# Scan rows behind the routing, first blocks' rows in the sorted rows' places, a last store on GpSimd, attention's additions later and in halves

## The chip, the cores and the metric

The kernel runs on one core of one Trainium2 chip. The metric is the time of one execution on the device in microseconds (us), the median of several runs. One core has a matrix engine (TensorE, PE in the profile, with its weight loads as PEld), a vector engine (VectorE, DVE), an engine for activation functions (ScalarE, ACT), a general engine (GpSimd, POOL) and one that issues transfers (SyncE, SP). Each works through its own list of instructions in order, and they meet through semaphores.

## The reference

The input x has 8 batches of 512 tokens with 256 numbers each, all float32. Four parts follow one another, each added to what went in:

```python
x = x + scan(layernorm(x))        # silu(x Win + b), a state that decays by 0.9, times Wout
x = x + ffn(layernorm(x))         # mixture of experts
x = x + attention(layernorm(x))   # causal, 16 heads of 16
x = x + ffn(layernorm(x))         # the same mixture of experts, same weights
```

```python
def ffn(x):
    topk_idx, tw = _route(x, router_w, bias)            # 4 of 16 experts for each token
    combine = (one_hot(topk_idx, E) * tw[..., None]).sum(1)
    h = einsum('td,edf->etf', x, gate_w)
    u = einsum('td,edf->etf', x, up_w)
    y = einsum('etf,efd->etd', silu(h) * u, down_w)
    routed = einsum('etd,te->td', y, combine)
    sh = silu(x @ sh_gate_w) * (x @ sh_up_w) @ sh_down_w    # shared experts, all tokens
    return routed + sh
```

The routing takes sigmoid scores, keeps the two best of four groups of experts, the four best experts in them, and scales the four scores to a sum of 2.5.

## The kernel before

Tokens lie on the 128 partitions, so a batch is a tile of 128 x 4 x 256. There are four long stages. The first (0 to 368 us) runs over the 8 batches with the scan (class Scan, L436), the routing of the batch before and the shared experts of the batch before that. The second (368 to 769) runs the routed experts in blocks of 128 sorted rows (routed, L765; 136 blocks). The third (769 to 1350) is the attention (class Attention, L965) with routing and shared experts of the second mixture in the same manner, the fourth (1350 to 1749) its blocks. Then the last sums go out, to 1776.

**Order inside a batch.** stretch (L1192) sets the order by hand. Each piece of work is a generator; beside takes a step from the piece that is least far, and timed gives a piece's steps the share of the batch at which each falls due. So a batch's instructions are one list, merged from the main product (pz, state, y, py in the scan), the normalizations, the routing (scores, choices), the sends of the rows and the shared experts. Tiles come from pools with a number of places per tag; an instruction that needs a place waits until the tile that had it before has been read.

**The routing's rows.** normed (L376) takes the mean and the variance of a batch on VectorE (L382, L383), raises the variance to the power -0.5 on GpSimd (L402), or on VectorE where by_vector is set, calls place for the tile, and writes four normalized row tiles on VectorE (L405). For the routing, place (L524) takes a tile of tag rows (two places; 4 x 272 numbers for a partition) and writes the token's number into its last columns with an iota on GpSimd (L526). So the iota waits until the transfers that read the tile's last holder have landed. These transfers are the sends (L665): 16 indirect transfers for each batch, issued by GpSimd, that put the rows where their experts' blocks begin to be read (xg). They follow the gain (L651), which VectorE writes into the same tile after the scores' product pr.

**The scan's chain.** For each of four columns of a batch PE makes pz, ScalarE its sigmoid, VectorE the product xi (L476), the running state (L478) and, after ScalarE's multiplication of xi, the output y (L482). The output product py (L421) needs the four y. All these stand on VectorE in one list with the rows of L405.

**The boundary.** The last shared sum of a stage is copied by ScalarE (L947) and stored by SP (L948). Then each engine loads a count (L889) and branches (L892): more blocks than 136 run only where they are needed. In this data they are not, and the untaken side adds to the semaphores what the taken side would have added, on SP and on GpSimd too. Then run (L869) loads the rows of the first two blocks (load, L792; SP's transfer at L796), and PE turns them (L811). The rows' tiles are in tag kb4 (nine places), which the shared experts, the transposes and many more share.

**The attention's inputs.** After the first mixture, x of a batch is the sum of two parts: the residual with every other block's sums, and the shared experts' with those of the rest. load_sum (L140) issues both loads on SP and one addition of 128 x 1024 on VectorE (L145). In a batch of the stretch it is called after the pieces of the routing are made and before beside merges them, so the addition stands at the head of the batch's list. The attention runs two batches ahead: when it starts, batches 0 and 1 lie ready (prepared, L1132), made beside the blocks, and batch 2 is loaded in its first batch. Its main product begins with pq, whose copies with a parity mask stand on VectorE (L1002).

Of the kernel before, what the change touches and what calls it, by code (L numbers as in the profile page):

```python
# [10 lines left out]
FP = mybir.dt.float32  # L11
AF = mybir.ActivationFunctionType
ALU = mybir.AluOpType
AX = mybir.AxisListType

P = 128
B, T, D = 8, 512, 256
# [57 lines left out]
def tile_hybrid_block(  # L75
# [64 lines left out]
    def load_sum(i: int, b: int, more, queue=nc.sync):  # L140

        x_sb = xpool.tile([P, NT, D], FP, tag="x", name=f"x{i}_{b}")
        queue.dma_start(out=x_sb, in_=rows_of(parts[i][0], b))
        queue.dma_start(out=more, in_=rows_of(parts[i][1], b))
        nc.vector.tensor_add(x_sb, x_sb, more)  # L145
        x_tiles[b] = x_sb


# [226 lines left out]

    def normed(b: int, tag: str, place, by_vector: bool = False):  # L376

# [26 lines left out]
        for t in range(NT):  # L404
            nc.vector.tensor_scalar(  # L405
                xn[:, t, :], x_sb[:, t, :], mv[:, t, 0:1], rstd[:, t : t + 1], ALU.subtract, ALU.mult
            )
            yield
# [24 lines left out]
    class Scan:  # L433
# [3 lines left out]

        norms, scores, choose = (0.08, 0.2, 0.32, 0.4), (0.48, 0.52, 0.61, 0.66), (0.71, 0.97)

        def load(self, b: int):  # L440
# [70 lines left out]

    counts = [region, region]
    upto = {}

    class Route:
# [8 lines left out]
        def place(self):  # L524
            rows = work.tile([P, NT, ROW], FP, tag="rows", name=f"sorted_{self.tag}")
            nc.gpsimd.iota(  # L526
                rows[:, :, D + 2 * TK :].bitcast(I32), [[P, NT], [0, 8]], base=self.b * T, channel_multiplier=1
            )
            self.held["rows"] = rows
            return rows[:, :, 0:D]  # L530

        def norm(self, by_vector: bool = False):
            return normed(self.b, self.tag, self.place, by_vector)

# [26 lines left out]
    def choices(i: int, b: int, tag: str, held, paced: bool):  # L561
# [81 lines left out]
        if not paced:  # L643
# [6 lines left out]
        nc.vector.reciprocal(den, den)  # L650
        nc.vector.scalar_tensor_tensor(  # L651
            rows[:, :, D : D + TK], gain, ROUTE_SCALE, den.unsqueeze(2).to_broadcast([P, NT, TK]), ALU.mult, ALU.mult
# [112 lines left out]
    def routed(i: int, table, beside):  # L765
# [3 lines left out]
        PE, SP = mybir.EngineType.PE, mybir.EngineType.SP  # L769
        held = {}  # L770

# [20 lines left out]
        def load(n: int):  # L792
            if n not in held:
                values(n)
            rows = work.tile([P, 4 * D], FP, tag="kb4", name=f"rows_{i}_{n}", bufs=KB)
            nc.sync.dma_start(out=rows[:, 0:ROW], in_=xg[i][bass.ds(held[n][1], BLK), :])  # L796
            held[n].append(rows)
# [70 lines left out]

        def run(first: int, last: int):  # L869
            load(first)  # L870
            load(first + 1)
            fetch(first)
            turn(first)
            for n in range(first, last + 2):
                if n + 2 < last:
                    load(n + 2)
                if n + 1 < last:
                    fetch(n + 1)
                if n < last:
                    up(n)  # L880
                if n + 1 < last:
                    turn(n + 1)
                if n - 2 >= first:
                    down(n - 2)
                    for work_beside in beside.get(n - 1, ()):
                        work_beside()
# [9 lines left out]
    def shared_experts(i: int, b: int, xnT_of, tanh: bool):  # L896
# [3 lines left out]
        def steps():  # L900
# [32 lines left out]
            for half in range(2):  # L933
# [13 lines left out]
                nc.scalar.copy(y_sb[:, 2 * half : 2 * half + 2, :], py)  # L947
            nc.sync.dma_start(out=rows_of(parts[i][1], b), in_=y_sb)  # L948

# [14 lines left out]
    class Attention:  # L964
        mixture, ahead, copies = 1, 2, by_both  # L965
        early = 2
        norms, scores, choose = (0.0, 0.12, 0.2, 0.28), (0.42, 0.46, 0.55, 0.6), (0.66, 0.95)

        def end(self):
# [3 lines left out]
        def load(self, b: int):  # L973
            load_sum(0, b, kb4(f"more0_{b}"))

# [156 lines left out]
    def prepared(b: int):  # L1132
# [17 lines left out]
        def begin():  # L1150
            x_sb = xpool.tile([P, NT, D], FP, tag="x", name=f"x0_{b}")
            more = free_home("v", f"more_{b}")
            for j, dst in ((1, more), (0, x_sb)):
                nc.gpsimd.dma_start(out=dst, in_=rows_of(parts[0][j], b))
            held.update(x=x_sb, more=more)

        def add():
            for t in range(0, NT, 2):
                rows = held["x"][:, t : t + 2, :]
                tc.keep_in_program_order(nc.vector.tensor_add(rows, rows, held["more"][:, t : t + 2, :]))  # L1160
            x_tiles[b] = held["x"]
            steps.append(normed(b, f"l1_{b}", place, by_vector=True))
# [29 lines left out]
    def stretch(layer):  # L1192
# [41 lines left out]
        for b in range(B):  # L1234
# [16 lines left out]
            if b > 0:  # L1251
                r = start_route(b - 1)
                if last:
                    pieces.append(timed(r.norm(), *spread(0.0, 0.12, NT), *spread(0.2, 0.28, NT)))
                else:
                    first, then, rows, full = layer.norms
                    pieces.append(timed(r.norm(), *spread(first, then, NT), *spread(rows, full, NT)))
# [12 lines left out]
            if nxt < B:  # L1270
                layer.load(nxt)
                pieces += [
                    timed(norm(nxt), *spread(0.32, 0.44, NT), *spread(0.56, 0.64, NT)),
                    timed(turn(nxt), 0.75, 0.79),
                ]
# [167 lines left out]
```

## Time and profile before

| what | us |
|---|---|
| median of 3 runs (1785.84 to 1786.67) | 1786.35 |
| the profiled execution | 1778.1 |
| its span | 1776.4 |
| PE busy in 0 to 50 | 28.50 |
| PE busy in 50 to 265 | 206.49 of 215 |
| PE busy in 265 to 300 | 26.33 of 35 |
| PE busy in 300 to 368 | 65.79 of 68 |
| PE busy in 368 to 375 | 0.88 of 7 |
| PE busy in 375 to 769 | 393.48 of 394 |
| PE busy in 780 to 790 | 1.39 of 10 |
| PE busy in 800 to 1349 | 538.81 of 549 |
| PE busy in 1349 to 1356 | 0.78 of 7 |
| PE busy in 1356 to 1749 | 391.91 of 393 |
| PE busy in 1749 to 1776.4 | 0.80 of 27.4 |

The page shows one profiled execution; the span is from its first to its last instruction. A group's row names line, engine, operation, what it writes and reads, and in brackets how long the engine idled before it and what ended that wait. A row of waits has the waiting engine and line, the one it waited for, total us, times and the longest. A row of windows has, after the window and its length, the busy time of PE, PEld, DVE, ACT and POOL with the instructions in brackets, then the granted clock of PE as a share of full speed, the share of the transfer engines and GB/s. A row of the timeline has the start and the duration in us.

### The profile page before, as it was taken

The page shows a single profiled execution, that of the slowest core. Times are in us where ns is not written, and L with a number is a line of the kernel's source. Part 1 is how long each engine was busy: PE and PEld are TensorE (multiplying, and loading weights), DVE is VectorE, ACT ScalarE, POOL GpSimd, SP SyncE. Part 2 cuts the span into 40 slices and gives each one's busy share as a digit, 9 for nine tenths or more (in the row PEclk, how much of TensorE's full clock was granted, in tenths as well). Part 3 has the DMA queues.
Part 4 walks back from the last instruction along what each step waited for, and adds up shares of the span by engine and source line. Part 5 has one row for each costly group of instructions (what it writes and reads, how often), then busy time and mean ns, then how long its engine had stood idle before and what let it go on. Part 6 is the DMA issues. An engine that isn't in the chain of part 4 may idle for free. (4 is left out here: it accounts for less than half of the span.)

```text
span 1776.4 us, 32812 instructions
## 1 busy us (share of the span) xinstructions
PE 1674.7 (94%) x10640; PEld 1253.8 (71%) x10640; DVE 1090.5 (61%) x3399; ACT 805.7 (45%) x1740; POOL 772.2 (43%) x675
## 2 busy tenths in 40 slices
PE   5999998989999999979999999999998999999994
PEld 3566664579999999954445455455466999999993
DVE  5977767435555655545776675766753665555552
ACT  2322222135555555535654554544523555555552
POOL 4255554625555655530021422312452555555663
PEclk9999998999999999989999999999999999999997
DMA  5443322535555655530012112112443555566766
GB/s 168 161 152 128 131 91 91 184 76 96 95 98 108 103 98 94 98 83 13 25 50 73 63 61 73 52 58 78 145 177 79 94 98 94 103 134 128 129 123 178
DMA packets 149998, 181.37 MB, mean 102 GB/s; under 512 B 16096, under 2 KB 136960, under 8 KB 149824
## 3 DMA queue, kind: packets, MB, share of 16 engines
q0 software_dynamic: 54432, 81.53, 24.1%
q1 hardware_dynamic: 93600, 93.50, 17.3%
q10 hardware_dynamic: 1792, 4.19, 0.6%
q8 instruction: 89, 1.46, 0.3%
q14 instruction: 85, 0.70, 0.1%
HBM read 81.62 MB, written 97.53 MB: 101 GB/s over the span
## 5 line engine op out<-in xcount | busy, mean ns | idle before, releaser
L859 POOL DMA_INDIRECT part<-rows x272 | 428.3, 1575 | 363.6 <-ACT rows L858 287.4
L665 POOL DMA_INDIRECT xg<-sorted_m,slots_m x256 | 256.5, 1002 | 279.4 <-ACT slots_m L662 115.5
L822 PEld LDWEIGHTS ph<-rows,gate 128*128 128x128 f32 x2176 | 285.9, 192 | 15.8 <-ACT rows L812 1.1
L822 PE MATMUL ph<-rows,gate 128*128 128x128 f32 x2176 | 289.3, 276 | 0.6 <-ACT rows L812 0.6
L822 PE MATMUL ph<-rows,up 128*128 128x128 f32 x2176 | 288.5, 276 | 0.0
L850 PE MATMUL pyr<-w_all,rows 128*128 x1088 | 280.4, 380 | 0.0
L822 PEld LDWEIGHTS ph<-rows,up 128*128 128x128 f32 x2176 | 266.0, 193 | 0.0
L830 ACT ACTIVATE rows<-ph 128x256 f32<-128x256 f32 x272 | 104.5, 384 | 328.7 <-PE ph L822 328.7
L831 DVE TENSOR_TENSOR rows<-ph,rows 128x256 f32<-128x256 f32 x272 | 115.3, 424 | 194.1 <-ACT rows L830 193.8
L850 PEld LDWEIGHTS pyr<-w_all,rows 128*128 128x128 f32 x1088 | 185.2, 191 | 14.2 <-ACT rows L858 0.4
L804 ACT COPY gate<-w_all 128x512 f32 x272 | 170.1, 627 | 14.7 <-SPq L892 2.5
L1057 ACT ACTIVATE w_all<-ps_a 128x1024 f32<-128x1024 f32 x128 | 124.4, 1021 | 80.2 <-PE ps_a L1046 74.1
L804 DVE COPY up<-w_all 128x512 f32 x272 | 119.5, 440 | 33.3 <-PE ph L822 18.1
L858 ACT ACTIVATE rows<-pyr,gain 128x256 f32<-128x256 f32 x272 | 128.6, 473 | 14.4 <-PE pyr L850 12.2
L1046 PE MATMUL ps_a<-w_all 32*128 32x512 f32 (+3 forms) x1024 | 122.1, 472 | 7.1 <-ACT w_all L1057 5.7
L911 PE MATMUL pg_m<-xT_m,su_sb 128*128 128x512 f32 x256 | 126.6, 617 | 0.8 <-DVE sig_m L929 0.8
L835 DVE SCALAR_TENSOR_TENSOR gain<-rows,expert_b 128x4 f32<-128x4 f32 x272 | 61.2, 225 | 103.8 <-ACT rows L858 84.2
L911 PE MATMUL pg_m<-xT_m,sg_sb 128*128 128x512 f32 x256 | 123.0, 603 | 0.0
L939 PE MATMUL pd_m<-sd_sb,act_m 128*128 128x256 f32 x512 | 120.5, 384 | 0.0
L832 DVE TENSOR_TENSOR rows<-ph,rows 128x256 f32<-128x256 f32 x272 | 115.1, 423 | 8.3
L811 PE MATMUL pt<-ident,rows 128*128 128x128 f32 x544 | 105.0, 275 | 13.4 <-DMA rows<-xg 13.1
L939 PEld LDWEIGHTS pd_m<-sd_sb,act_m 128*128 128x128 f32 x512 | 96.1, 191 | 21.1 <-issue 4.7
(219 smaller groups left out, 2203.0 us busy)
## 6 DMA issues: line engine op xcount, KB each, us to landing
rows<-xg SPq DMA_DIRECT2D x272, 136.0 KB, 2.6
part<-x SPq DMA_DIRECT2D x16, 512.0 KB, 3.0
part<-ys_m SPq DMA_DIRECT2D x16, 512.0 KB, 3.0
w_all<-in_L_ffn_gate_w_dram SPq DMA_DIRECT2D x24, 256.0 KB, 5.4
w_all<-in_L_ffn_up_w_dram SPq DMA_DIRECT2D x24, 256.0 KB, 4.8
w_all<-in_L_ffn_down_w_dram SPq DMA_DIRECT2D x24, 256.0 KB, 5.6
sum<-part POOLq DMA_DIRECT2D x10, 512.0 KB, 3.9
xg<-zeros SPq DMA_DIRECT2D x34, 136.0 KB, 2.3
```

Of the source, the lines that this page charges most:

```text
L665: nc.gpsimd.indirect_dma_start(out=xg[i], out_offset=bass.IndirectOffsetOnAxis(ap=slots[:, at : at + 1], axis=0), in_=rows[:, t, :], in_of ...
L804: copy(here, w_all[:, bass.ds(held[n][0] + half * KD * F, KD * F)])
L822: nc.tensor.matmul(ph[:, s, f * P : (f + 1) * P], lhsT=both[s][:, k * F + f * P : k * F + (f + 1) * P], rhs=rows[:, ROW + k * P : ROW + (k ...
L831: nc.vector.tensor_mul(act, ph[:, 0, :], act)
L832: nc.vector.tensor_mul(act, ph[:, 1, :], act)
L850: nc.tensor.matmul(py, lhsT=act[:, f * P : (f + 1) * P], rhs=w_all[:, bass.ds(w + 2 * KD * F + f * D, D)], start=(f == 0), stop=(f == KF - 1),
L858: nc.scalar.mul(rows[:, 0:D], py, gain[:, TK : TK + 1])
L859: nc.gpsimd.indirect_dma_start(out=parts[i][n % 2], out_offset=bass.IndirectOffsetOnAxis(ap=rows[:, D + 2 * TK : D + 2 * TK + 1].bitcast(U ...
L911: nc.tensor.matmul(dst, lhsT=w[:, k, f * P : (f + 1) * P], rhs=xnT[:, k, :], start=(k == 0), stop=(k == KD - 1),)
L939: nc.tensor.matmul(py[:, j, :], lhsT=acts[n][:, f, t * P : (t + 1) * P], rhs=shared[n][3][:, f, :], start=(n == 0 and f == 0), stop=(n == ...
L1046: nc.tensor.matmul(ps[j // 2][:, j % 2, col : col + n], lhsT=k_sb[w][r, o, c * P : (c + 1) * P], rhs=q_sb[r, o, c * P : T], start=True, st ...
L1057: nc.scalar.activation(es[two], ps[two][:, :, 0:cols], AF.Exp, scale=ATT_SCALE)
```

## The change

Five edits:

- normed takes a function past. For the routing of the first mixture it gives the instruction that wrote the gain of the batch before (L651, kept in gained), and each of the four rows of L405 is issued after it in the order. For the first batch and for the second mixture there is nothing to stand behind. The iota of place keeps its place in program order, which puts it after the power on GpSimd.
- In the last batch of a stretch the rows fall due at last_rows: 0.26 to 0.33 in the scan; in the attention 0.2 to 0.28, as before.
- The first two blocks of each run take their rows' tiles from tag rows, the sorted rows' places; the others from kb4 as before.
- The shared sum of the last batch is stored by GpSimd, the others' by SP.
- load_sum issues the loads (the shared part first) and returns the addition as two steps of 512 columns; in the attention's stretch these fall due at 0.24 and 0.28 of the batch. prepared uses the same function on GpSimd's queue.

The diff, without the import of nullcontext:

```diff
@@ -140,10 +140,18 @@
     def load_sum(i: int, b: int, more, queue=nc.sync):
 
         x_sb = xpool.tile([P, NT, D], FP, tag="x", name=f"x{i}_{b}")
+        queue.dma_start(out=more, in_=rows_of(parts[i][1], b))
         queue.dma_start(out=x_sb, in_=rows_of(parts[i][0], b))
-        queue.dma_start(out=more, in_=rows_of(parts[i][1], b))
-        nc.vector.tensor_add(x_sb, x_sb, more)
         x_tiles[b] = x_sb
+
+        def added():
+
+            for t in range(0, NT, 2):
+                rows = x_sb[:, t : t + 2, :]
+                tc.keep_in_program_order(nc.vector.tensor_add(rows, rows, more[:, t : t + 2, :]))
+                yield
+
+        return added()
 
 
     load_x(0)
@@ -373,7 +381,7 @@
     by_both = (nc.scalar.copy, nc.vector.tensor_copy)
     by_scalar = (nc.scalar.copy, nc.scalar.copy)
 
-    def normed(b: int, tag: str, place, by_vector: bool = False):
+    def normed(b: int, tag: str, place, by_vector: bool = False, past=lambda: None):
 
         x_sb = x_tiles[b]
         stats = small.tile([P, NT, 6], FP, tag="stats", name=f"stats_{tag}")
@@ -402,9 +410,10 @@
             nc.gpsimd.tensor_tensor(rstd, rstd, neg_half, ALU.pow)
         xn = place()
         for t in range(NT):
-            nc.vector.tensor_scalar(
-                xn[:, t, :], x_sb[:, t, :], mv[:, t, 0:1], rstd[:, t : t + 1], ALU.subtract, ALU.mult
-            )
+            with tc.issue_after(past().ins) if past() is not None else nullcontext():
+                nc.vector.tensor_scalar(
+                    xn[:, t, :], x_sb[:, t, :], mv[:, t, 0:1], rstd[:, t : t + 1], ALU.subtract, ALU.mult
+                )
             yield
 
     def kb4(name: str):
@@ -436,6 +445,7 @@
 
 
         norms, scores, choose = (0.08, 0.2, 0.32, 0.4), (0.48, 0.52, 0.61, 0.66), (0.71, 0.97)
+        last_rows = (0.26, 0.33)
 
         def load(self, b: int):
             if b + 1 < B and b > 0:
@@ -510,6 +520,7 @@
         return sel
 
     counts = [region, region]
+    gained = {}
     upto = {}
 
     class Route:
@@ -523,14 +534,19 @@
 
         def place(self):
             rows = work.tile([P, NT, ROW], FP, tag="rows", name=f"sorted_{self.tag}")
-            nc.gpsimd.iota(
-                rows[:, :, D + 2 * TK :].bitcast(I32), [[P, NT], [0, 8]], base=self.b * T, channel_multiplier=1
+            tc.keep_in_program_order(
+                nc.gpsimd.iota(
+                    rows[:, :, D + 2 * TK :].bitcast(I32), [[P, NT], [0, 8]], base=self.b * T, channel_multiplier=1
+                )
             )
             self.held["rows"] = rows
             return rows[:, :, 0:D]
 
         def norm(self, by_vector: bool = False):
-            return normed(self.b, self.tag, self.place, by_vector)
+
+
+            past = (lambda: gained.get(self.b - 1)) if self.i == 0 else lambda: None
+            return normed(self.b, self.tag, self.place, by_vector, past=past)
 
         def scores(self):
             yield from turned(
@@ -648,7 +664,7 @@
         nc.vector.tensor_reduce(den, gain, AX.X, ALU.add)
         nc.vector.tensor_scalar(den, den, 1e-20, None, ALU.add)
         nc.vector.reciprocal(den, den)
-        nc.vector.scalar_tensor_tensor(
+        gained[b] = nc.vector.scalar_tensor_tensor(
             rows[:, :, D : D + TK], gain, ROUTE_SCALE, den.unsqueeze(2).to_broadcast([P, NT, TK]), ALU.mult, ALU.mult
         )
 
@@ -767,7 +783,7 @@
         weight_at, row_at, expert, many, _ = table
         ACT, DVE = mybir.EngineType.Activation, mybir.EngineType.DVE
         PE, SP = mybir.EngineType.PE, mybir.EngineType.SP
-        held = {}
+        held, first_of = {}, [0]
 
         def values(n: int):
 
@@ -792,7 +808,12 @@
         def load(n: int):
             if n not in held:
                 values(n)
-            rows = work.tile([P, 4 * D], FP, tag="kb4", name=f"rows_{i}_{n}", bufs=KB)
+            if n - first_of[0] < 2:
+
+                rows = work.tile([P, NT, ROW], FP, tag="rows", name=f"rows_{i}_{n}")
+                rows = rows.rearrange("p t c -> p (t c)")[:, 0 : 4 * D]
+            else:
+                rows = work.tile([P, 4 * D], FP, tag="kb4", name=f"rows_{i}_{n}", bufs=KB)
             nc.sync.dma_start(out=rows[:, 0:ROW], in_=xg[i][bass.ds(held[n][1], BLK), :])
             held[n].append(rows)
 
@@ -867,6 +888,7 @@
             )
 
         def run(first: int, last: int):
+            first_of[0] = first
             load(first)
             load(first + 1)
             fetch(first)
@@ -945,7 +967,8 @@
                             )
                     yield NSH * KF * D
                 nc.scalar.copy(y_sb[:, 2 * half : 2 * half + 2, :], py)
-            nc.sync.dma_start(out=rows_of(parts[i][1], b), in_=y_sb)
+
+            (nc.gpsimd if b == B - 1 else nc.sync).dma_start(out=rows_of(parts[i][1], b), in_=y_sb)
 
         return Piece(NSH * KF * (2 * KD * T + NT * D), steps())
 
@@ -965,13 +988,14 @@
         mixture, ahead, copies = 1, 2, by_both
         early = 2
         norms, scores, choose = (0.0, 0.12, 0.2, 0.28), (0.42, 0.46, 0.55, 0.6), (0.66, 0.95)
+        last_rows = (0.2, 0.28)
 
         def end(self):
             for e in range(first_expert, E):
                 load_expert(e)
 
         def load(self, b: int):
-            load_sum(0, b, kb4(f"more0_{b}"))
+            return load_sum(0, b, kb4(f"more0_{b}"))
 
         def project(self, b: int, xnT):
             tag = f"a{b}"
@@ -1148,17 +1172,11 @@
 
 
         def begin():
-            x_sb = xpool.tile([P, NT, D], FP, tag="x", name=f"x0_{b}")
-            more = free_home("v", f"more_{b}")
-            for j, dst in ((1, more), (0, x_sb)):
-                nc.gpsimd.dma_start(out=dst, in_=rows_of(parts[0][j], b))
-            held.update(x=x_sb, more=more)
+            held["added"] = load_sum(0, b, free_home("v", f"more_{b}"), nc.gpsimd)
 
         def add():
-            for t in range(0, NT, 2):
-                rows = held["x"][:, t : t + 2, :]
-                tc.keep_in_program_order(nc.vector.tensor_add(rows, rows, held["more"][:, t : t + 2, :]))
-            x_tiles[b] = held["x"]
+            for _ in held["added"]:
+                pass
             steps.append(normed(b, f"l1_{b}", place, by_vector=True))
 
         def step(many: int):
@@ -1251,7 +1269,7 @@
             if b > 0:
                 r = start_route(b - 1)
                 if last:
-                    pieces.append(timed(r.norm(), *spread(0.0, 0.12, NT), *spread(0.2, 0.28, NT)))
+                    pieces.append(timed(r.norm(), *spread(0.0, 0.12, NT), *spread(*layer.last_rows, NT)))
                 else:
                     first, then, rows, full = layer.norms
                     pieces.append(timed(r.norm(), *spread(first, then, NT), *spread(rows, full, NT)))
@@ -1268,7 +1286,9 @@
                         timed(some(r.rest, PICKS), *spread(*layer.choose, PICKS)),
                     ]
             if nxt < B:
-                layer.load(nxt)
+                added = layer.load(nxt)
+                if added is not None:
+                    pieces.append(timed(added, 0.24, 0.28))
                 pieces += [
                     timed(norm(nxt), *spread(0.32, 0.44, NT), *spread(0.56, 0.64, NT)),
                     timed(turn(nxt), 0.75, 0.79),
```

## The prediction

> **What bounds the kernel now.** I read the page's first two parts, then TensorE's waits, then the windows of the stages, then each stall in order of time.
>
> ```profile
> span 1776.4 us, 32812 instructions
> PE 1674.7 (94%) x10640; PEld 1253.8 (71%) x10640; DVE 1090.5 (61%) x3399; ACT 805.7 (45%) x1740; POOL 772.2 (43%) x675
> ```
>
> TensorE is busy for 1674.7 of 1776.4 us. No edit touches a matmul, so what can be won is its 101.7 us of idle time, and the slow clock after an idle stretch. The waits of PE say who ends that time (total, times, longest):
>
> ```profile
> PE pt_l L368 <- DVE xn L405: 16.0, 4, 15.0
> PE pt L811 <- DMA rows<-xg: 13.1, 4, 6.2
> PE py_s L421 <- DVE y_s L482: 9.2, 6, 2.0
> PE pl_m L549 <- ACT xT_m L370: 9.2, 2, 7.5
> PE pt_l L368 <- DVE w_all L1002: 8.6, 1, 8.6
> ...
> PE pt_m L368 <- DVE sorted_m L405: 3.9, 2, 2.1
> ```
>
> The first row is nearly all the kernel's start (15.0), untouched. The others are the change's targets: two boundaries into the experts' blocks (13.1), the scan's output product (9.2), the last scan iteration (7.5 of 9.2), the first attention batch (8.6). The page's chain of waits starts at 1353 us, so it says nothing of the first three stages. In the windows the columns that matter are PE busy and PEclk, the granted clock:
>
> ```profile
> 265.00:300.00 35.00, 26.33 (x80) 15.20 (x79) 21.72 (x67) 9.41 (x23) 15.47 (x16) 0.80 0.23 86
> ...
> 780.00:790.00 10.00, 1.39 (x9) 1.01 (x12) 3.28 (x9) 0.61 (x2) 0.00 (x0) 0.63 0.53 164
> 790.00:800.00 10.00, 8.57 (x42) 2.68 (x40) 5.43 (x15) 6.56 (x8) 2.20 (x3) 0.86 0.00 1
> ```
>
> The two places of low clock are those after the two longest stalls. Two timelines of VectorE show the head of each queue:
>
> ```profile
> 191.03 1.38 DVE L405 TENSOR_SCALAR sorted_m<-x,mv_m,rstd_m 128x256 f32<-128x256 f32 x4 [7.18 <-POOL rstd_m L402]
> ...
> 786.72 1.23 DVE L145 TENSOR_TENSOR x<-x,more 128x1024 f32<-128x1024 f32 x1 [12.48 <-DMA more<-part]
> 787.87 0.75 DVE L1002 TENSOR_SCALAR w_all<-pq_a,parity 128x512 f32<-128x512 f32 x1
> ```
>
> In both, ready work stands behind an instruction that waits.
>
> **What the Trainium skill says.** "Advanced Engine Details and Errata", Sequencer and Instruction Queues: an engine's instructions go into one queue and there wait for their semaphores; the trace agrees (12.48 us of wait, L1002 behind it). "TensorE: Matmul & The Clock Gate", What's actually happening: the array falls to half clock after an idle window of about 3.4 us and needs a busy one to recover; the trace agrees in kind (8.61 us idle, then 0.63 and 0.86). "DMA: Bandwidth & Descriptors", Issuing engines are not separate DMA queues: issuing from another engine saves only the issue time on the sequencer; here 0.38 us on SP, 0.83 us on GpSimd for the same 512 KB (L1154). The price of the halved addition: "VectorE: DVE Perf Modes", the TRN2 errata, gives (N+151)/0.96 ns for a float32 tensor_tensor, so 1.22 us at 1024 and 0.69 at 512; the trace has 1.23, and 0.68 at 512 (L930).
>
> **Part 1, attention's additions.** Before, load_sum puts the 1024-wide addition of x0_2 at the point where its loads are issued. Those follow the last scatter-adds of the experts, so VectorE stands from 774.2 to 786.72. Behind it is L1002 (0.75 us), and PE, having reached its transposes at 780.05, waits for it until 788.67: 8.61 us. After, the additions are a piece due at 0.24 to 0.28 of the batch. In the order after, L1002 comes directly after the L1002 ahead of it, at 774.2, and the first half of x0_2's addition stands behind the L1002 that ran at about 806, so at about 798 once the stall is gone. The data lands at 786.7, 11 us before: no wait. Cost: six additions become twelve, 6 x (2 x 0.68 - 1.23) = 0.8 us of an engine that is 61% busy, hidden beside PE. The clock: 10 us at 0.86 is up to 1.4 us; I take 0.5, as ScalarE holds PE there too (6.56 us busy). Later batches: VectorE's other waits for x<-part (15.8 us in 5) go, but PE idles there 0.1 to 0.5 us each: 0 to 2 us, taken as 0. Part 1: -9 (bounds -7.5, -12).
>
> **Part 2, scan rows behind the routing.** Before, in an iteration (the one from 183.4, period 40.72 us), VectorE has the variance at 183.85 and waits 7.18 us: GpSimd is sending the rows of an earlier batch to 188.10, its iota (L526) waits for these to land until 189.81, then comes the power to 190.99. All of the scan's work is queued behind the four rows. After, the rows follow the gain of the batch before (L651), one at each step, and the iota comes after the power and after the first sends. I stepped the new VectorE order through the measured durations, with PE where it was:
>
> - Without rows ahead, the first xi starts at 186.03, not 192.33. The routing's sums then wait for PE's pr (190.83) and ScalarE (191.14), so 0.8 us of the 6.3 are lost; the gain ends at 198.87 instead of 204.4, 5.5 us earlier.
> - Then xi_3, row 1 (0.35), state_3 (1.22), rows 2 to 4, to 202.72; y_3 at 202.71 to 203.46, earlier than 208.59.
> - PE wants the rows' transposes at 201.0 to 201.4 and waits some 1.4 us there; its old wait of 1.75 us for y_3 (206.9 to 208.65) is gone. Net -0.35 in the two steady iterations; the fourth gains 1.2 (it had 0.85 and 1.75), the third loses 0.9 (it had 0.55), the second loses 1.5 (it had none). Together -0.5 for five iterations. Each hand-made position is good to about 1 us, so -4 to +5; I take 0.
>
> Last iteration: VectorE waits 7.25 us for the rows' rstd at 272.44, its first xi is at 273.74; PE stands from 278.94 to 286.45 (7.51 us, pl_m for ScalarE's xT_m copies, which stand in ScalarE's queue behind products of the scan). After, VectorE runs 6.3 us earlier; rows end at about 282.7, PE transposes to 283.2, and xT_m, now behind xi_3's product, comes at 284.5: PE starts pl 2.0 us earlier, with its idle time cut in pieces. In that stage 35 us at a clock of 0.80 hold some 4 us of slow matmuls (14 pl in 3.01 us against 1.85 elsewhere); I take 0.5 of it. So -2.5 (bounds 0, -5).
>
> Behind it: sorted_m0_7 waited 3.33 us on VectorE for the last send of m0_5 to land (about 314.2; sends 286.56 to 307.80), PE then 2.06 us (312.8 to 314.9), and a slow clock (8 transposes in 2.21 us against 1.04). These sends hang on the gain and start some 6 us earlier, so land at 308, before rstd at 310.9. -2.06 and 0.5 of clock: -2.5 (bounds 0, -3.5). Part 2: -5 (bounds -9, +5).
>
> **Part 3, the two boundaries.** Before: PE ends at 368.32, ScalarE's copy at 368.95, SP's store to 369.35, SP's TensorLoad L889 at 369.4, branch 369.7, its semaphores to 370.5, L782 some 1.1 us, the first rows' load at 372.07, landed 374.42; PE idle 6.12 us, 6.22 at the second (load 1353.43). After, the store and its wait stand on GpSimd, and SP reaches the load early. But rows_0 and rows_1 now lie in the tag of the sorted rows, which GpSimd's sends read and which the untaken branch's blocks also use: the load waits for GpSimd's semaphore increment at that branch's end, and GpSimd is behind the store. Its chain: copy 368.95, store 0.83, TensorLoad 0.33 to 0.76, branch 0.3, increment 1.0 to 1.6 (the rows of L892): 371.4 to 372.4, around 372.0. That is what SP took. Gain 0 to 0.7 each; I take 0.4. If GpSimd's increment counts at its start the load goes at 370.4: -1.6 each; if GpSimd's branch is slower than SP's, +0.7. Part 3: -1 (bounds -3.5, +1.5). The tail from 1749 on (27.4 us) is untouched.
>
> **Sum.** -9 -5 -1 = -15 on the profiled execution (1778.1 us, 1.7 of it outside the span): 1763. That one is 8.25 us (0.46%) below the median 1786.35; taken off the median, 1771.3, say 1771.5.
>
> **Rivals.**
> - Attention only: the rows' wait on PE takes back what the scan gains, GpSimd's increment takes what SP gives up. For: 1.4 us in each iteration stands on a hand-made position. Against: the last iteration's stall hangs on VectorE's 7.25 us. 1786.35 - 9 = 1777.4.
> - More: clock and stalls of 265 to 315 all recovered (-9) and boundaries free of GpSimd (-3 each): -24, 1762.5. For: SP's path holds 3 us after the copy. Against: the chain above.
> - Slower: the rows behind the gain starve PE. Place: PE's transposes at 201 in each iteration. If the gain stays at 204.4, because the routing's sums hang on PE and ScalarE rather than on the rows ahead, the rows end at 208.3 and PE waits 7.3 us instead of 1.75: 5 x 5.5 = 28, plus 2 at the last iteration, less 10: +20, 1806. It decides from 3 us per iteration on (5 x 3 = 15), a gain at 201.9. Against: before, pr and ScalarE are ready at 191, 13 us ahead of the gain.
> - No change: the addition still waits at its new place (a later landing) or L1002 is held by another wait, scan neutral: 1785.
>
> **Chances.** Forecast 0.54 (own range 1767 to 1775.5), attention only 0.24, more 0.11, slower 0.06, no change 0.05. About 0.2% (3.6 us) is what a measurement can tell. Faster 0.89, same 0.05, slower 0.06. The range to hold 8 in 10 covers the forecast, most of attention only and a part of more: 1763 to 1780.
>
> **What would show it.** Right: no VectorE wait over 2 us for x<-part at the start of attention, PE's wait for L1002 gone; sorted_m's wait for rstd_m (39.8 us in 9) nearly gone, pt_m's wait for sorted_m grown from 3.9 to about 8, py_s's for y_s from 9.2 to under 2; pl_m's 7.5 at about 5; the first load still some 3 us after the last copy, with GpSimd's increment just ahead of it. Wrong: pt_m's wait above 20, or the idle time at 780 elsewhere by another name.

## The result, and the profile after

The changed kernel takes 1766.89 us (median of 4 runs, 1764.67 to 1771.96) against 1786.14 for the one before: a ratio of 0.9893 with a 95% interval of 0.9878 to 0.9909, so 19.3 us (16 to 22) less. The forecast was 1771.5, within 1763 to 1780; the narrower range of the outcome that was called the forecast began at 1767, just above what was measured.

The head of the changed kernel's page:

```profile
span 1766.9 us, 32836 instructions
PE 1678.8 (95%) x10640; PEld 1254.8 (71%) x10640; DVE 1094.7 (62%) x3405; ACT 808.3 (46%) x1740; POOL 776.5 (44%) x677
```

Its waits of PE (engine and line that wait, what for, total us, times, longest; the lines of the code have moved by 8 to 24):

```profile
PE pt_l L376 <- DVE xn L414: 17.0, 4, 15.5
PE pt L832 <- DMA rows<-xg: 15.6, 8, 5.8
PE pt_m L376 <- DVE sorted_m L414: 9.8, 8, 3.2
...
PE py_s L430 <- DVE y_s L492: 3.0, 2, 2.0
PE pl_m L565 <- ACT xT_m L378: 2.1, 2, 1.7
```

The 8.6 us for L1002 is gone, pl_m's 9.2 is 2.1, and py_s's 9.2 is 3.0; pt_m's wait for the sorted rows has grown from 3.9 to 9.8. The loads of the rows cost more in all than before, with four more waits, though the longest is shorter: of that below.

The span changed by 9.5 us in these two profiles and the median by 19.3, so the whole must be cut before it is read. Here it is cut at PE's own instructions (the first pz of an iteration, the last pd_m of a stage, the first pt of the blocks, the first pv of an attention batch), in us, with a second profile of the kernel before (before_again, span 1786.6) beside it:

| stretch | before | before_again | after |
|---|---|---|---|
| start to the third iteration | 63.87 | 64.72 | 65.99 |
| third to last iteration | 200.95 | 202.03 | 199.50 |
| last iteration to the stage's end | 103.50 | 102.19 | 96.58 |
| first boundary, PE idle | 6.12 | 6.11 | 5.79 |
| first blocks, to attention's first pv | 401.56 | 402.45 | 401.53 |
| first attention batch | 49.52 | 49.49 | 39.29 |
| six batches | 357.39 | 357.45 | 357.43 |
| last batch to the stage's end | 166.75 | 167.10 | 168.80 |
| second boundary, PE idle | 6.22 | 6.13 | 5.26 |
| second blocks | 393.91 | 398.19 | 399.05 |
| tail | 26.56 | 30.74 | 27.66 |

The five stretches that the change was to act on give 1.45 + 6.92 + 0.33 + 10.23 + 0.96 = 19.9 us (19.5 against before_again). The others give back 10.4 in this pair of profiles and nothing (-0.2) against before_again, so most of the 10.4 differs from run to run. The medians, 19.3 us apart, lie beside the 19.9.

### The profile page after: what moved, and what is told of

Its sections match the earlier page's. It is cut to its first block, busy times and chain, and to the rows that moved or that the text cites. A ratio compares the mean times of both kernels' runs of the same rounds, so it can differ in the third digit from the quotient of the medians.

```text
span 1766.9 us, 32836 instructions
## 1 busy us (share of the span) xinstructions
PE 1678.8 (95%) x10640; PEld 1254.8 (71%) x10640; DVE 1094.7 (62%) x3405; ACT 808.3 (46%) x1740; POOL 776.5 (44%) x677
## 4 chain that ended last, share of the span: by engine, by line
PE 46%; DMA 4%; issue 1%; DVE 1%; ACT 1%; POOL 1%; ACTq 0%; SPq 0%; POOLq 0%; DVEq 0%
PE ph L843 13%; PE pyr L871 6%; PE pg_m L933 5%; PE ps_a L1070 5%; PE po_a L1105 4%; PE pd_m L961 2%; PE pq_a L1015 2%; PE pt L832 2%; PE pv_a L1033 2%; PE py_a L430 2%; DMA part<-rows 1%; DMA xg<-sorted_m,slots_m 1%; PE pl_m L565 1%; PE pto_a L1121 1%; POOL xg L681 1%
```

## The experiments

The runs fall in three groups. Each group ran on one chip, with the kernel before beside it: 1802.87 us in the first, 1784.26 in the second, 1787.15 in the third. Ratios are to that one; they and their intervals stand as on record, and the quotient of the medians can differ from them by 0.002. Only stretches of the same chip are compared, unless it is said otherwise; of the kernel before there is a trace in the second group alone.

**1. The parts, each alone, and the whole again (first group).** In attn_only, the kernel before gets the new load_sum and its timed steps (due at 0.24 and 0.28 of the batch) alone; two lines of the diff:

```diff
-        nc.vector.tensor_add(x_sb, x_sb, more)
+        return added()
```

> Only the attention's additions of the change (later, in halves, the shared part loaded first), all else as before. Theory: the head of VectorE's list is what PE waits for at the start of attention, so the 8.6 us wait for L1002 goes and the clock after it stays up; in the changed kernel's trace the first attention batch was 10.2 us shorter, so 9 to 10.5 us less than before, scan and boundaries unmoved. Rival (the loads are late anyway and the wait returns under another name in that batch): under 4 us less.

Ratio 0.9921 (0.9891 to 0.9951): 14 us less, with an interval of 5 to either side that takes in the 9 to 10.5 expected. The first attention batch takes 39.28 us, as in the changed kernel, where bound_only and scan_only, without this part, take 49.34 and 49.59 on this chip. The rival falls. The later place, the halves and the order of the two loads were not tried apart.

In scan_only, past, the iota's place and last_rows alone:

```diff
+            past = (lambda: gained.get(self.b - 1)) if self.i == 0 else lambda: None
+            return normed(self.b, self.tag, self.place, by_vector, past=past)
```

> Only the scan's part: rows behind the gain, iota in program order, the last batch's rows at 0.26 to 0.33. Theory: VectorE's wait for GpSimd's power was at the head of its list; the last scan iteration and what follows it give nearly all, 6 to 7 us, the iterations before about 0.8 us each where PE had 1.75 and now has 0.84, less about 1 us each where it had none: 6 us less than before in all, with a spread of 2 from the start. Rival (PE waits for the rows instead of y, a zero sum): within 1.5 us of before.

0.9955 (0.9930 to 0.9979): 8 us less (4 to 13), where 6 were expected. Third to last iteration: 199.49, against 204.10 in attn_only and 203.65 in bound_only, so the stretches show 4 to 5 of the 8. But the last iteration to the stage's end took 110.35, and 110.64 and 110.03 without the scan's part. On this chip that stretch is some 7 to 13 us longer than on the others in every kernel, and nothing is won in it, although its long wait falls here too, from 6.75 us to pieces of 3.19, 1.00 and 0.46. The waits behind it are of the same kind with and without the scan's part (pd_m for act_m, pr_m for sel_m); why this chip has them is open.

In bound_only, the first two blocks' tiles and the last store alone:

```diff
-            nc.sync.dma_start(out=rows_of(parts[i][1], b), in_=y_sb)
+            (nc.gpsimd if b == B - 1 else nc.sync).dma_start(out=rows_of(parts[i][1], b), in_=y_sb)
```

> Only the first two blocks' places and the last store on GpSimd. Theory: GpSimd's increment after the untaken branch gates the first load, so PE's idle time at the boundaries falls from 6.12 and 6.22 to about 5.8 and 5.3: 1.3 us less in all. Rival (SP's list was the gate, and is free now): both idle times below 4 us, 5 us less or more.

1.0007 (0.9992 to 1.0022). PE idles 5.70 and 5.16 us: 1.4 less together than in attn_only (6.11 and 6.16), too little for these runs to show. The rival falls: neither idle time is below 4 us, and 5 us would have shown.

> The changed kernel once more, unedited. In its first trace the second experts' stage took 399.0 us against 393.9 before, with four waits of PE for rows<-xg between 1585 and 1628. If that stretch belongs to the change, it is here again and the time is near 1768; if it is chance of the transfers, it is shorter or elsewhere, and the time is near 1764.

0.9905 (0.9875 to 0.9936); on this slower chip the expected 1768 and 1764 can't be told apart by the time. The second blocks took 399.29 us again, and the waits are back. PE's timeline of after_again:

```profile
1605.83 0.41 PE L832 MATMUL pt<-ident,rows 128*128 128x128 f32 x2 [0.35 <-DMA rows<-xg]
1610.08 0.41 PE L832 MATMUL pt<-ident,rows 128*128 128x128 f32 x2 [1.19 <-DMA rows<-xg]
1643.76 0.41 PE L832 MATMUL pt<-ident,rows 128*128 128x128 f32 x2 [1.93 <-DMA rows<-xg]
1647.44 0.41 PE L832 MATMUL pt<-ident,rows 128*128 128x128 f32 x2 [0.62 <-DMA rows<-xg]
```

The stage starts at 1360.46 here and at 1340.18 in the first trace, so these stand 245 to 287 us behind its start, as they do there (1585 to 1627). In iota_only the four are at the same places. The other kernels have waits for rows near these places too, but fewer or shorter ones: one of 0.53 us in the kernel before, one of 1.93 in before_again, two in bound_only, three in scan_only. The four profiles whose iota stands as before (two of the kernel before, attn_only, bound_only) have 393.9 to 398.2 us in this stage (mean 395.7). Four with the iota in program order (the changed kernel twice, scan_only, iota_only) have 396.4 to 399.3 (mean 398.3); six more, which change the boundary further, have 397.7 to 403.3. So perhaps 2.6 us of the gain are given back late in the second blocks. The ranges overlap, and the kernel before in its second profile is within 0.9 us of the changed one, so this is not shown. By what way an iota's place in the attention's list, or in the scan's, could reach a load of rows there was not tried and stays open.

**2. What holds the first load at a boundary (second group).** Before, SP was late, behind its own store and branch:

```profile
368.97 0.38 SPq L948 DMA_DIRECT2D part<-ys_m  x1
372.07 7.17 SPq L796 DMA_DIRECT2D rows<-xg  x9
374.44 0.66 PE L811 MATMUL pt<-ident,rows 128*128 128x128 f32 x2 [6.12 <-DMA rows<-xg]
```

In the changed kernel, the timeline of all engines shows who is late:

```profile
362.11 0.59 ACT L969 COPY ys_m<-pd_m 128x512 f32<-128x512 f32 x1 [1.53 <-PE pd_m L961]
362.99 0.92 POOL L971 DMA_DIRECT2D part<-ys_m  x1 [10.49 <-ACT ys_m L969]
...
365.50 3.73 SPq L817 DMA_DIRECT2D rows<-xg  x5
367.84 0.22 DVE L856 SCALAR_TENSOR_TENSOR gain<-rows,expert_b 128x4 f32<-128x4 f32 x1 [3.70 <-DMA rows<-xg]
367.87 0.66 PE L832 MATMUL pt<-ident,rows 128*128 128x128 f32 x2 [5.79 <-DMA rows<-xg]
```

and the rows of the branch's line (count, shortest, median and longest in ns, first and last start in us) give GpSimd's part of it:

```profile
L914 SPq EVENT_SEMAPHORE  x16: 17/17/17, 343.1 to 1316.8; - x16
...
L914 POOLq INC_SWDGE_SEM  x2: 654/828/1002, 364.3 to 1336.7; - x2
```

SP is through the branch at 343, 19 us before PE ends. GpSimd's increment starts at 364.3 and takes 1.00 us, and SP's load goes at 365.50, 0.2 us behind it. Three edits tell the tie apart. First, the rows in kb4, with the store still on GpSimd:

```diff
-            if n - first_of[0] < 2:
-                rows = work.tile([P, NT, ROW], FP, tag="rows", name=f"rows_{i}_{n}")
-                rows = rows.rearrange("p t c -> p (t c)")[:, 0 : 4 * D]
-            else:
-                rows = work.tile([P, 4 * D], FP, tag="kb4", name=f"rows_{i}_{n}", bufs=KB)
+            rows = work.tile([P, 4 * D], FP, tag="kb4", name=f"rows_{i}_{n}", bufs=KB)
```

> The changed kernel with all blocks' rows in tag kb4 again, the store still on GpSimd. Theory: the place in tag rows is what ties the first load to GpSimd's increment; without it the load waits for nothing of GpSimd, goes when PE ends, and PE's idle time at a boundary falls from 5.8 and 5.3 to some 3 us; but rows_1 gets the place of the last sum, so it waits for that store to land (issue 363.0, some 4.3 us), and gives about 1 us of it back as a second wait. 2 to 5 us less than the changed kernel. Rival (the branch on the other engines is the gate): idle times unchanged, same time.

PE's timeline:

```profile
358.72 2.11 PE L956 MATMUL pd_m<-sd_sb,act_m 128*128 128x256 f32 x9
364.20 0.66 PE L827 MATMUL pt<-ident,rows 128*128 128x128 f32 x2 [3.37 <-DMA rows<-xg]
368.33 0.66 PE L827 MATMUL pt<-ident,rows 128*128 128x128 f32 x2 [3.47 <-DMA rows<-xg]
```

The first wait falls to 3.37 us (2.24 at the second boundary). Without the place in tag rows nothing of GpSimd holds it: the load goes at 360.86, as PE ends, and GpSimd's increment starts only at 363.05. But the second block's rows now have the last sum's place, and wait until its store has landed: 3.47 and 4.39 us more, where about 1 was expected. Ratio 0.9893 (0.9869 to 0.9918), the same as the changed kernel's in the result (it did not run in this group), and not the 2 to 5 us less that were expected. Second, each block where it is free:

```diff
-            if n - first_of[0] < 2:
+            if n - first_of[0] == 1:
```

> The changed kernel with only the second block's rows in tag rows, the first block's in kb4. Theory: the first load is free of GpSimd and the second of the store's landing, so both lie in time: PE's idle time at each boundary some 3 us or less, no second wait, 4 to 6 us less than the changed kernel. Rival (the branch gates): same time.

```profile
361.67 1.89 PE L961 MATMUL pd_m<-sd_sb,act_m 128*128 128x256 f32 x8
364.95 0.41 PE L832 MATMUL pt<-ident,rows 128*128 128x128 f32 x2 [1.39 <-DMA rows<-xg]
367.16 0.41 PE L832 MATMUL pt<-ident,rows 128*128 128x128 f32 x2 [1.80 <-DMA rows<-xg]
```

1.39 and 1.43 us at the boundaries, less than expected, and 1.80 once behind the first (1.52 in two pieces behind the second), where no second wait was expected. Ratio 0.9853 (0.9826 to 0.9879), by the medians 6.5 us better than first_kb4. The branch itself was never the gate: the first load goes at 362.73, and GpSimd's increment starts at 365.78. Nor is it tag rows as such, for the second block lies in tag rows here and its load goes at 363.57, before the increment as well. As the code reads, the difference is who had the place before. The untaken branch's blocks come first in the program. In the changed kernel its first two take both places of tag rows, and the blocks that run take them over from these; here the branch takes one place, and the second block gets the other, from the sorted rows. No run changes this alone. Third, the store on ScalarE, with both tiles in tag rows:

```diff
-            (nc.gpsimd if b == B - 1 else nc.sync).dma_start(...)
+            (nc.scalar if b == B - 1 else nc.sync).dma_start(...)
```

> The changed kernel with the last store issued by ScalarE instead of GpSimd. Theory (GpSimd's increment gates, because it is behind the store): GpSimd is done with the branch long before, the first load goes some 0.5 to 1 us after ScalarE's copy, and PE idles some 4.0 us at a boundary: 2.5 to 3.5 us less than the changed kernel, part of it given back as the gate copies stand behind the store's issue. Rival (the place in tag rows alone holds it): idle times as in the changed kernel.

```profile
363.09 0.58 ACT L969 COPY ys_m<-pd_m 128x512 f32<-128x512 f32 x1 [1.53 <-PE pd_m L961]
363.70 0.38 ACTq L971 DMA_DIRECT2D part<-ys_m  x1
...
365.27 7.01 SPq L817 DMA_DIRECT2D rows<-xg  x9
366.32 1.14 ACT L825 COPY gate<-w_all 128x512 f32 x2 [2.65 <-DVE up L825]
```

PE idles 4.60 and 4.55 us, 0.6 more than expected, and the gate copies start 2.65 us after ScalarE's last copy. The load goes 1.6 us after that copy's end instead of 2.8: GpSimd was the gate, and ScalarE, whose count after the branch (at 365.13) the load also waits for, is the next one. Ratio 0.9880 (0.9857 to 0.9903): the 2.5 to 3.5 us less than the changed kernel can't be told from nothing.

> The kernel before, unedited, for a second trace. Its profiled execution was 1778.1 us, its timed runs 1786. If the experts' stages vary by chance of the transfers, the second one is 394 to 402 us here, with PE's waits for rows<-xg spread over it, and the scan and attention stages agree with the first trace within 1 us.

1.0004 (0.9989 to 1.0020). As expected in the second blocks (398.19) and the attention (49.49); the scan has 3.2 us more in one iteration and 2.0 less in the next, so not within 1 us in every stretch. Its sum to the stage's end is 0.2 us less than in the first profile, counted from the third iteration.

**3. What in the scan's part does it (third group).** The iota's new place alone:

```diff
-            nc.gpsimd.iota(rows[...], ...)
+            tc.keep_in_program_order(nc.gpsimd.iota(rows[...], ...))
```

> The kernel before with the iota kept in program order (after the power on GpSimd) as its only edit; the rows stay ahead of the scan's work on VectorE, at their old due times. Theory (the place of the rows in VectorE's list is what counts): the power still waits for the sends ahead of it, VectorE still waits some 5.4 of its 7.2 us, so the last scan iteration gains at most 2 of its 7.5 us, 2 us less than before up to its end and some more in the iterations, 2 to 6 us in all. Rival (the iota's wait for the landing is what held the power, the move of the rows is not needed): the time of the scan part alone, 8 us less.

0.9964 (0.9944 to 0.9984): 6.4 us less (3 to 10). The interval holds both the 2 to 6 of the theory and the rival's 8, so the trace has to tell them apart. VectorE's timeline:

```profile
188.53 1.38 DVE L419 TENSOR_SCALAR sorted_m<-x,mv_m,rstd_m 128x256 f32<-128x256 f32 x4 [5.92 <-DMA xg<-sorted_m,slots_m]
189.82 0.74 DVE L491 SCALAR_TENSOR_TENSOR xi_s<-pz_s,b_in_sb,xi_s 128x512 f32<-128x512 f32 x1
```

The head of the list still waits, for 5.92 us instead of 7.18, and now for the landing itself. The 1.26 us are nearly what PE lacked: its wait for y is 0.56 to 1.10 us where it was 1.75, and third to last iteration take 195.6 us, less than with the whole change. The last iteration's long stall stays (6.88 us), as the theory had it: the head of the list still counts there, and the gain is in the iterations.

The same question with the rest of the change in place and the better boundary; the rows ahead again:

```diff
-            past = (lambda: gained.get(self.b - 1)) if self.i == 0 else lambda: None
+            past = lambda: None
-        last_rows = (0.26, 0.33)
+        last_rows = (0.2, 0.28)
```

> The kernel with the first block's rows in kb4 and the second's in the sorted rows' places, attention's additions late and in halves, the iota in program order, but the scan's rows ahead of the scan's work as before and the last batch's at 0.2 to 0.28. Theory: it lacks what the rows' new place gives after the last iteration (5.7 us between its start and the end of the stage, on the chip of the second call), and PE waits for y instead of the rows in each iteration: 4 to 6 us more than first_split. Rival (the iota alone does it): within 1.5 us of first_split or below it.

> first_split once more, for the two others of this call on the same chip: PE's idle time at the boundaries about 1.4 us again, 5 us less than the changed kernel.

split_front 0.9873 (0.9842 to 0.9903), split_again 0.9862 (0.9836 to 0.9887): 1 to 2 us apart, which these intervals can't tell from nothing, and not 4 to 6. The stretches say why: third to last iteration 197.3 against 199.5, last iteration to the end 100.8 against 96.5. The rows' new place costs 2.2 us in the iterations and gives 4.3 after them; against iota_only, with 195.6 and 102.3, it costs 3.9 and gives 5.8 (one iteration of split_front has a piece at half clock). Boundaries in split_again: 1.49 and 1.42, as expected.

Then the iterations' cost is only a matter of due times, if PE's transposes can be later:

```diff
-        norms, scores, choose = (0.08, 0.2, 0.32, 0.4), (0.48, 0.52, 0.61, 0.66), (0.71, 0.97)
+        norms, scores, choose = (0.08, 0.2, 0.32, 0.4), (0.51, 0.55, 0.63, 0.68), (0.72, 0.97)
```

> first_split with the scores of the scan's routing due later (0.51, 0.55, 0.63 to 0.68 instead of 0.48, 0.52, 0.61 to 0.66). If PE's wait of 0.84 us for the last sorted row in each of five iterations is only a matter of where the transposes stand, it goes: 4 us less than first_split. Rival (VectorE's whole list sets the iteration, so that another wait takes its place): same time, the wait at py or pl.

Windows inside the iterations (window, its length, then the busy time of PE, PEld, DVE, ACT, POOL; granted clock; transfers):

```profile
110.00:150.00 40.00, 40.00 (x153) 25.93 (x152) 31.94 (x97) 11.90 (x28) 21.34 (x23) 1.00 0.45 158
150.00:190.00 40.00, 40.00 (x153) 25.88 (x152) 31.93 (x100) 12.56 (x28) 21.32 (x23) 1.00 0.39 139
190.00:230.00 40.00, 40.00 (x154) 25.81 (x153) 31.94 (x97) 13.02 (x29) 21.34 (x23) 1.00 0.40 138
```

PE has no idle time left in the iterations: each takes 38.40 us, where the changed kernel has 39.9 and the kernel before 38.4 to 41.7. No other wait took the place in them. Ratio 0.9830 (0.9806 to 0.9853): 1756.84 us, the best of all, and 30 us less than the kernel before on that chip. Against split_again the median is 6.5 us less, where 4 were expected; the stretch itself gives 7.5 (192.0 against 199.5), for each wait of 0.84 us that is gone takes 1.5 us of its iteration with it. The rows ahead of the scan's work with these later due times were not tried.

## Why the prediction was right, point by point

- **Attention: -9 forecast, -10.2 measured.** VectorE's timeline in the changed kernel:

```profile
770.32 0.75 DVE L1026 TENSOR_SCALAR w_all<-pq_a,parity 128x512 f32<-128x512 f32 x1 [2.68 <-ACT w_all L1025]
773.93 0.69 DVE L378 COPY xT_l<-pt_l 128x512 f32<-128x512 f32 x1 [2.85 <-PE pt_l L376]
...
789.63 0.75 DVE L1026 TENSOR_SCALAR w_all<-pq_a,parity 128x512 f32<-128x512 f32 x1
790.29 0.68 DVE L151 TENSOR_TENSOR x<-x,more 128x512 f32<-128x512 f32 x1
```

The first addition stands behind a later L1026, without a wait, as forecast, and nothing came in place of the 8.61 us. (The L1026 at 770.32 waits 2.68 us for ScalarE, which the forecast's place for it left out; it is done before PE comes to its transposes at 772.85.) The clock's share was sized at 0.5 us. What is left of the 10.23 beside the 8.61 is 1.6: there is no stall and the clock stays up, and eight matmuls of ps_a that took 2.09 us behind the stall take 1.14:

```profile
783.00:793.00 10.00, 9.63 (x73) 3.72 (x74) 7.64 (x21) 6.45 (x9) 0.00 (x0) 1.00 0.01 2
```

VectorE's waits for x<-part in the later batches, which were to go, did not (15.1 us in 5, 15.8 before); they were taken as 0, and PE shows no change there.

- **The scan's iterations: 0 forecast, -1.5 measured** (-2.5 against before_again). Where the list's new positions were worked out by hand, they came out so. The iteration looked at is 2.3 us later here:

```profile
201.21 0.17 DVE L667 SCALAR_TENSOR_TENSOR sorted_m<-choices_sm,den_m 128x16 f32<-128x16 f32 x1
202.55 0.40 DVE L414 TENSOR_SCALAR sorted_m<-x,mv_m,rstd_m 128x256 f32<-128x256 f32 x1
204.00 1.03 DVE L414 TENSOR_SCALAR sorted_m<-x,mv_m,rstd_m 128x256 f32<-128x256 f32 x3
204.96 0.74 DVE L492 SCALAR_TENSOR_TENSOR y_s<-state_s,bc_sb,xi_s 128x512 f32<-128x512 f32 x1
```

Less 2.32, the gain ends at 199.06 (forecast 198.87) and the last row at 202.71 (forecast 202.72). Mis-sized was PE's new wait: 0.84 us, not 1.4, in each of five iterations (0.91 in the first). But a wait also costs more than its idle time, which the forecast left out. PE's timeline of the kernel before and, behind the dots, of the changed one:

```profile
201.02 0.60 PE L368 MATMUL pt_m<-ident,sorted_m 128*128 128x128 f32 x4
201.45 1.88 PE L911 MATMUL pg_m<-xT_m,sg_sb 128*128 128x512 f32 x4
...
203.34 0.27 PE L376 MATMUL pt_m<-ident,sorted_m 128*128 128x128 f32 x1
204.44 0.97 PE L376 MATMUL pt_m<-ident,sorted_m 128*128 128x128 f32 x3 [0.84 <-DVE sorted_m L414]
205.25 1.02 PE L933 MATMUL pg_m<-xT_m,sg_sb 128*128 128x512 f32 x2
```

From the first of these four transposes to the next pg_m it is 0.43 us before and 1.91 after: 0.84 us of idle time cost 1.5. In the same way the wait of 1.75 us for y made iterations of 40.7 us out of 38.4. So the two steady iterations gain 0.8 us each, not 0.35. The forecast's own terms for the five iterations, with its signs, add up to +0.5 and not to the -0.5 that it states; it took 0, so nothing hangs on this.

- **Last iteration and behind it: -5 forecast, -6.9 measured** on the chip of the two first profiles and -5.7 between the second group's before_again and first_split, but nothing on the first group's chip. PE's timeline there, of the kernel before and of the changed one:

```profile
286.45 0.61 PE L549 MATMUL pl_m<-rw_sb,xT_m 128*128 128x16 f32 x2 [7.51 <-ACT xT_m L370]
...
281.31 1.54 PE L376 MATMUL pt_m<-ident,sorted_m 128*128 128x128 f32 x6 [3.19 <-DVE sorted_m L414]
283.40 0.69 PE L376 MATMUL pt_m<-ident,sorted_m 128*128 128x128 f32 x2 [0.54 <-DVE sorted_m L414]
284.55 0.61 PE L565 MATMUL pl_m<-rw_sb,xT_m 128*128 128x16 f32 x2 [0.46 <-ACT xT_m L378]
```

The iteration starts 0.67 us later here, so pl starts at 283.9 in the time of the kernel before (forecast 284.5), and the 7.51 us are 3.19 + 0.54 + 0.46. pt_m of the last batch waits for nothing at 310.44, as forecast. Against the first profile the clock gives more than its term: the windows have 1.00 from 300 on, where the kernel before had 0.83 between 310 and 320. In before_again the time at half clock in this stretch is that of the changed kernel (13.7 us each), so this part isn't sure to belong to the change. Against before_again the stretch is 5.6 us shorter and PE's idle time in it 5.3.

- **Which edit of the scan's part does it.** The prediction put the gain down to the rows that leave the head of VectorE's list, and in these runs this is the smaller part. From the third iteration to the stage's end the kernel before took 304.5 and 304.2 us in its two traces, neither from the third group. In that group the iota's place alone brings it to 297.9, and with the rest of the change, all but the rows' place, to 298.1 (split_front); the rows' new place brings it to 296.0 (split_again). At these due times the move takes in the iterations half or more of what it gives behind them. With the later scores of split_later it is 288.5. The rows' move without the iota's was not tried, so the shares hold for this order of the two edits only.

- **Boundaries: -1 forecast, -1.3 measured**, for the reason given: the load waits for GpSimd's increment. GpSimd's chain was 0.5 us shorter than summed, as its TensorLoad starts with the store's issue and not behind it: the increment ends 2.6 us after the copy's end, not 3.1.

- **The whole.** The three sums are 5 us short (-15, and -19.9 measured), and it is in the scan (3.4 of it) and the clock of attention (1.2). That the stages between stay as they are held for the first blocks and for the attention's batches between the first and the last; for the second blocks it is open (5.1 us more than in the first profile, 0.9 more than in before_again). The rivals: "attention only" and "slower" fell with the iterations, "no change" with the first batch. "More" had the boundaries wrong, and 6.9 of its 9 us came between 265 and the stage's end. The measured 1766.89 lies between the forecast and "more".

## What to carry to other kernels

An engine's list is a queue, so the first thing to look for is an instruction at its head that waits, with ready work behind it that the bounding engine needs; what that is worth is read from the bounding engine's wait, not from the length of the stall ahead (VectorE's 12.5 and 7.2 us were 8.6 and 1.75 of PE's). A wait of the bounding engine in the midst of its work can cost more than its idle time (0.84 us were 1.5 here). A buffer's place carries its history: the first load at a boundary was tied to other engines' counts after a branch because its place had last belonged, as the code reads, to a block of the side not taken, and a choice of place for each tile was worth more than moving the store. After moving work, look at the new wait once more: 1 to 3% of the iteration in a few due times took away the last idle time that the move had left in the iterations.

## What the runs showed of the hardware that was not expected

- The granted clock falls in pieces: in the traces it is 1.00 or 0.50, and in the kernel before 0.50 for 3.4, 6.8, 10.2 or 13.7 us at a time (26.5 in the idle tail). In each of the 14 traces all pieces begin on one grid of 3.41 us, to within 0.02 us. A piece can follow as little as one idle time of 0.92 us (at 1264 in the kernel before), and the same idle times don't always bring one: in the first attention batch PE waits 0.5, 0.4 and 0.9 us, and in after_again and split_again a piece follows and the batch takes 40.50 and 40.67 us, in the changed kernel and attn_only none follows and it takes 39.29 and 39.28. So the idle window of about 3.4 us that the prediction quotes is not needed for a piece. A stall of 8.61 us cost 10.2.
- The same kernel's median differed by chip from 1784.26 to 1802.87 us. Most of it lies after the last scan iteration and in the last attention batch: 13 and 8 us more in after_again than in the changed kernel's first profile. An edit's gain there (6.9 us on one chip) was absent on another.
- On GpSimd the instruction after a transfer's issue starts while the issue runs (TensorLoad at 362.98 beside the store of 362.99 to 363.91).
